# Graph network on one core: the last chunk of messages finished in three steps, the last block's sums added in PSUM

## The chip, the core and the metric

The kernel runs on one core of a Trainium2 chip. Its time is the device time of one execution in microseconds; before the change it is 4211.55 us, the median of three runs (4207.63 to 4215.61).

## What is computed

Four layers of a graph network on 6250 nodes with 64 features and 206250 edges, which come sorted by destination. Each layer normalises the node rows (mean, variance, ReLU) and adds its result to the rows `x`. The first two layers were left as they are. The change is in the third and at the seam between the third and the fourth.

```python
# third: messages along edges, averaged (as a power mean) at their destination
scale = sigmoid(mlp(E) @ Bw + Bb);  shift = mlp(E) @ Cw + Cb
M     = clip(scale * Vp[src] + shift, EPS) ** 2
x     = x + sqrt(segment_sum(M, dst) / max(count, 1))
# fourth: h = relu(layernorm(x)); three propagations with the same graph
embs = acc = h
for _ in range(3):
    embs = segment_sum(norm[:, None] * embs[row], col)
    acc  = acc + embs
x = x + acc / 4
```

## The kernel before

**Nodes and counts.** Nodes are padded to 49 blocks of 128, in seven chunks of seven blocks (`NB`, `CB`, `NC`). The graph stands in DRAM as a matrix of edge counts in fp8, one tensor `A[c]` for each chunk c of destination nodes: 128 partitions by 49 blocks of source nodes by 896 columns. A piece is 7 blocks of it, 784 KB. Node values go to TensorE as three bf16 parts each (`U3`: 128 x 49 x 3 x 64), so that their sum has nearly f32 precision; `split` makes the parts.

**The message stage** (lines 1383 to 1666). Edges are worked in 202 groups of 1024 (`G`), in a software pipeline of 208 slots: `slot(i)` starts group i (POOL gathers its source values by eight indirect DMAs, `fetched`), passes earlier groups through two small layers, gates, clips and squares group i-4, sums group i-5 by destination on TensorE, and adds group i-6 to the node sums `H` (`added_to_nodes`). Gathered values have four buffers; line 1559 of group i-4 frees the one that group i's gather fills. The order of PE, ScalarE and VectorE in this stage is the order of the program text; SP and POOL are ordered by the scheduler.

Beside this, each slot does some items of a list, `todo`, which `some_of` works off: (1) `crossed`, a comparison. It shows that the count matrix is symmetric: three or four 128 x 128 products turn blocks of a piece, and VectorE compares them with the mirrored piece (`there`) in line 1435. There are 392, 14 for each pair of chunks. (2) `partial`, a sum. It is a part of the first propagation of the fourth layer, done early: seven blocks of source nodes, already finished, are multiplied by 448 destination columns (`spread`, 21 products) and added to `Y` in line 1454. (3) `here`, the load of a piece one item ahead. Comparisons, sums and the squared messages (`p_m`, lines 1566 to 1638) share the two PSUM buffers `p_sum`. In slot i, n = ceil(items left / slots to the next end) items are done, n - n//2 ahead of `squared` and n//2 near the slot's end (lines 1620, 1621 and 1640). The ends are the slots in which chunks of nodes are complete: 35, 64, 93, 122, 151, 180 and 207.

Up to slot 35 the list holds four pairs of chunks (`FIRST`): 56 comparisons and 4 loads. When chunk c is complete, `finished(c)` averages, takes the root, adds to `X`, normalises, splits into `U3`, and then plans the next period (`CROSS[c]`): four pairs with 56 comparisons, and 14 sums over seven loads, 77 items. Chunk 5's period is slots 181 to 207. Chunk 6 plans nothing; it is finished in slot 207.

**The first propagation** (lines 1703 to 1715). Chunk 6's own part of the sums is done after the messages: for each of seven destination chunks, two sums of 21 products, two adds to `Y`, then seven f32 products (`to_nodes`, line 741) that turn `Y` into node rows, and `propagated`, five VectorE and two ScalarE instructions that scale the rows, add them to `H` and split them for the next pass.

**The second and third propagation** are `gather`: for each destination chunk 7 pieces, 343 products with 192 columns each (line 1195), four reductions and `propagated`. Six pieces are buffered. The product on piece k needs chunk k of the values split before.

Of the kernel before, what the change touches and what calls it, by code (L numbers as in the profile page):

```python
# [8 lines left out]
F32 = mybir.dt.float32  # L9
# [4 lines left out]
OP = mybir.AluOpType  # L14
AX = mybir.AxisListType

P = 128
N = 6250
D = 64
# [598 lines left out]
def fast(ctx, tc, bad, x, src, dst, edge_attr, W3, b3, W4, b4, w1, b1, w2, b2, Bw, Bb, Cw, Cb,  # L618
# [52 lines left out]
    missed = const.tile([P, 3], F32, name="missed")  # L671

    def blocks(c):
        return slice(c * CB, (c + 1) * CB)

    def over_features(v, n=CB):
        return v.unsqueeze(2).to_broadcast([P, n, D])
# [14 lines left out]

    def normed(h, X_c):

        m = stat.tile([P, CB], F32, name="m")
        nc.vector.tensor_reduce(m, X_c, axis=AX.X, op=OP.add)
        nc.vector.tensor_scalar_mul(m, m, 1.0 / D)
        nc.vector.tensor_sub(h, X_c, over_features(m))
        q = stat.tile([P, CB, D], F32, name="q")
        nc.vector.tensor_mul(q, h, h)  # L700
        v = stat.tile([P, CB], F32, name="v")
        nc.vector.tensor_reduce(v, q, axis=AX.X, op=OP.add)
        nc.scalar.activation(v, v, AF.Sqrt, bias=eps, scale=1.0 / D)
        nc.vector.reciprocal(v, v)
        nc.vector.scalar_tensor_tensor(h, h, 0.0, over_features(v), op0=OP.max, op1=OP.mult)

    def of_nodes(pool):

# [1 line left out]

    def split(u, U3, c):
        u3 = U3[:, blocks(c), :, :]
        nc.scalar.activation(u3[:, :, 0, :], u, AF.Copy)
        r = stat.tile([P, CB, D], F32, name="r")
        nc.vector.tensor_sub(r, u, u3[:, :, 0, :])
        nc.scalar.activation(u3[:, :, 1, :], r, AF.Copy)
        nc.vector.tensor_sub(u3[:, :, 2, :], r, u3[:, :, 1, :])
# [455 lines left out]

    def normed_and_split(h, U3, c, scale):
        normed(h, X[:, blocks(c), :])
        u = stat.tile([P, CB, D], F32, name="u")
        nc.vector.tensor_mul(u, h, over_features(scale[:, blocks(c)]))
        split(u, U3, c)

    def gather(apool, wpool, psum, U3, then, beside=iter(())):  # L1180


        zeros = wpool.tile([P, 6 * D], BF16, name="zeros", bufs=1)
# [1 line left out]
        for c in range(NC):  # L1185
            p = [psum.tile([P, 512], F32, name=f"p_acc{q}") for q in range(4)]
            for k in range(NC):
                t = apool.tile([P, CB, W], COUNT, name="piece")
                nc.sync.dma_start(t, A[c][:, blocks(k), :])
                for d in range(CB):  # L1190
                    if k == 0 and d % 2 == 0:
                        nc.tensor.matmul(p[d // 2][:, :6 * D], ident_b, zeros,
                                         start=True, stop=False)
                    for b in range(CB):
                        nc.tensor.matmul(  # L1195
                            p[d // 2][:, d % 2 * 3 * D:(d % 2 + 1) * 3 * D],
                            t[:, b, d * P:(d + 1) * P],
                            U3[:, k * CB + b, :, :].rearrange("p t f -> p (t f)"),
                            start=False, stop=(k == NC - 1 and b == CB - 1 and d in (1, 3, 5, 6)))
                for _ in range(2 - (c > 0 or k > 4)):  # L1200
                    next(beside, None)
# [181 lines left out]
    with ExitStack() as ph:  # L1383
# [10 lines left out]

        CROSS = (((0, 6), (0, 1), (0, 2), (0, 0)), ((1, 6), (1, 2), (1, 3), (1, 1)),
                 ((2, 6), (2, 3), (2, 4), (2, 2)), ((3, 6), (3, 4), (3, 5), (3, 0)),
                 ((4, 6), (4, 5), (4, 0), (4, 1)), ((5, 6), (5, 0), (5, 1), (5, 2)))
        FIRST = ((3, 3), (4, 4), (5, 5), (6, 6))
        unlike = cpool.tile([P, 28 * 2 * CB], F32, name="unlike")

        def order(pairs):
            ks = [k for _, k in pairs]
            return [(pairs[0][0], k)
                    for k in ks + [k for k in range(NC) if (pairs[-1][0], k) not in pairs]]

        here_of = list(FIRST) + [at for pairs in CROSS for at in order(pairs)]
        there_of = list(FIRST) + [at for pairs in CROSS for at in pairs]
        held = {}

        def here(n):  # L1410

            if n < len(here_of):
                i, k = here_of[n]
                t = held["here", i, k] = piece_pool.tile([P, CB, W], COUNT, name="piece")
                nc.sync.dma_start(t, A[k][:, blocks(i), :])

        def there(n):

# [23 lines left out]
        def partial(i, s):  # L1442

            t = held["here", i, s // 2]
            p = ps_a.tile([P, 512], F32, name="p_sum", bufs=2)
            for b in range(CB):
                spread(p, U3, i * CB + b, t[:, b, s % 2 * CW:(s % 2 + 1) * CW], CW,
                       i * CB, CB)

            def added():  # L1450
                if i == 0:
                    nc.vector.tensor_copy(Y[:, s, :], p[:, :CW])
                else:
                    nc.vector.tensor_add(Y[:, s, :], Y[:, s, :], p[:, :CW])

            return added

        todo, crossings, asked = [], [], []

        def plan(pairs, sums):  # L1460
            for at, (i, k) in enumerate(order(pairs) if sums else pairs):
                asked.append((i, k))
                todo.append((here, len(asked)))
                if at < len(pairs):
# [21 lines left out]
                if then:  # L1486
                    read.append(then)

        def finished(c):

            t = H[:, blocks(c), :]
            nc.vector.tensor_mul(t, t, over_features(n1[:, blocks(c)]))

            nc.vector.tensor_scalar_max(t, t, 1e-30)
            nc.scalar.activation(t, t, AF.Sqrt)
            nc.vector.tensor_mul(t, t, over_features(some[:, blocks(c)]))
            nc.vector.tensor_add(X[:, blocks(c), :], X[:, blocks(c), :], t)
            normed_and_split(H[:, blocks(c), :], U3, c, norm3)
            if c < NC - 1:
                plan(CROSS[c], True)  # L1500

        here(0)
        there(0)
        plan(FIRST, False)
        last = {b: g for g in range(G) for b, _, _ in halves(g)}
        ends = [last[c * CB + CB - 1] for c in range(NC)]

        BC_AT, M_AT, SUM_AT, ADD_AT = 3, 4, 5, 6
        of = [{} for _ in range(G)]
        ends = [e + ADD_AT for e in ends]

        def loaded(g):
            of[g]["e"] = mpool.tile([P, J * D], F32, name="e", bufs=6)
# [70 lines left out]
        def added_to_nodes(g):  # L1587
# [5 lines left out]
            for k, (b, q0, q1) in enumerate(halves(g)):  # L1593
# [4 lines left out]
                else:  # L1598
                    nc.vector.tensor_scalar(H[:, b, :], r, part, None, op0=OP.mult)
                    begun.add(b)  # L1600
            return [b // CB for b, _, _ in halves(g) if last[b] == g and b % CB == CB - 1]

        def slot(i):
            def at(later):
# [12 lines left out]
            read_them()  # L1617
            if at(1):
                layer(i - 1, w1_d, "eT", "p_1")
            n = -(-len(todo) // max(min(k for k in ends if k >= i) + 1 - i, 1))  # L1620
            some_of(n - n // 2)
            if at(M_AT):
                squared(i - M_AT)
# [16 lines left out]
            some_of(n // 2)  # L1640
            if at(SUM_AT):
                summed(i - SUM_AT)
            for c in done:
                finished(c)

        for g in range(4):
            loaded(g)
# [2 lines left out]
                slot(i)  # L1650
            read_them()

        assert not todo and len(crossings) == 28 * 2 * CB


        nc.vector.tensor_reduce(missed[:, 2:3], unlike, axis=AX.X, op=OP.add)
# [14 lines left out]
    with ExitStack() as ph:  # L1671
# [2 lines left out]
        psum = ph.enter_context(tc.tile_pool(name="ps4", bufs=1, space=PSUM, reuse_waits="tile"))  # L1674
        upool = ph.enter_context(tc.tile_pool(name="upool", bufs=1, reuse_waits="tile"))

        for layer in range(3):
            V3 = of_nodes((upool, node)[layer]) if layer < 2 else None

            def propagated(c, y):  # L1680
                z = wpool.tile([P, CB, D], F32, name="z")
                s3 = over_features(norm3[:, blocks(c)])
                nc.vector.tensor_mul(z, y, s3)
                if V3 is not None:
                    u = wpool.tile([P, CB, D], F32, name="u")
                    nc.vector.tensor_mul(u, z, s3)
                    split(u, V3, c)
                h = H[:, blocks(c), :]
                nc.vector.tensor_add(h, h, z)
                if V3 is None:  # L1690
                    o = X[:, blocks(c), :]
                    nc.vector.scalar_tensor_tensor(o, h, 0.25, o, op0=OP.mult, op1=OP.add)
                    lo, hi = c * W, min((c + 1) * W, N)
                    full = (hi - lo) // P
                    nc.sync.dma_start(
                        out[lo:lo + full * P, :].rearrange("(b p) f -> p b f", p=P),
                        o[:, :full, :])
                    if lo + full * P < hi:
                        nc.sync.dma_start(out[lo + full * P:hi, :], o[:hi - lo - full * P, full, :])

            if layer:
                gather(apool, wpool, psum, U3, propagated)
            else:
                for s in range(CS):
                    if s % 2 == 0:
                        whole = apool.tile([P, CB, W], COUNT, name="piece")
                        nc.sync.dma_start(whole, A[s // 2][:, blocks(NC - 1), :])
                    t = whole[:, :, s % 2 * CW:(s % 2 + 1) * CW]
                    p = psum.tile([P, 512], F32, name="p_sum", bufs=2)
                    for b in range(CB):  # L1710
                        spread(p, U3, NB - CB + b, t[:, b, :], CW, NB - CB, CB)
                    nc.vector.tensor_add(Y[:, s, :], Y[:, s, :], p[:, :CW])
                    if s % 2:
                        propagated(s // 2, to_nodes(
                            psum, Y[:, s - 1:s + 1, :].rearrange("p s w -> p (s w)"), CB))
            U3 = V3


def gnn_kernel(tc, *args):
# [38 lines left out]
```

## Time and profile before

| | us |
|---|---|
| median of three runs | 4211.55 |
| the profiled execution: time, span | 4226.45, 4224.1 |
| graph, degrees, first two layers: to the first gated group | 1054.6 |
| message stage, first gated group to the end of chunk 6's finish | 1054.6 to 3764.9 |
| first propagation's last part | 3764.3 to 3809.6 |
| second and third propagation | 3809.6 to the end |
| busy: PE, VectorE, ScalarE, POOL | 3145.3, 2075.1, 1238.6, 1611.6 |

Times of stages are counted from the span's start. The engines are named as the profile has them: PE and PEld are TensorE's products and weight loads, DVE is VectorE, ACT is ScalarE, POOL is GpSimd, SP issues most DMAs. In the page's groups a row gives line, engine, operation, output and inputs, how many; then busy time and the mean ns of one; then the idle time of the engine just ahead of them and what ended it.

### The profile page before, as it was taken

The page shows a single profiled execution, that of the slowest core. Times are in us where ns is not written, and L with a number is a line of the kernel's source. Part 1 is how long each engine was busy: PE and PEld are TensorE (multiplying, and loading weights), DVE is VectorE, ACT ScalarE, POOL GpSimd, SP SyncE. Part 2 cuts the span into 40 slices and gives each one's busy share as a digit, 9 for nine tenths or more (in the row PEclk, how much of TensorE's full clock was granted, in tenths as well). Part 3 has the DMA queues.
Part 4 walks back from the last instruction along what each step waited for, and adds up shares of the span by engine and source line. Part 5 has one row for each costly group of instructions (what it writes and reads, how often), then busy time and mean ns, then how long its engine had stood idle before and what let it go on. Part 6 is the DMA issues. An engine that isn't in the chain of part 4 may idle for free.

```text
span 4224.1 us, 60998 instructions
## 1 busy us (share of the span) xinstructions
PE 3145.3 (74%) x24478; PEld 2248.4 (53%) x24478; DVE 2075.1 (49%) x5101; ACT 1238.6 (29%) x2061; POOL 1611.6 (38%) x1894
## 2 busy tenths in 40 slices
PE   2899989996665666766676676766766766689999
PEld 1788889994333333333333343433333333359999
DVE  6999935322544554454545454545444444562111
ACT  3677700001333322332323232323332332320000
POOL 5000010003666655655555554555555655510000
PEclk9999999997777778777777777778778777889999
DMA  3244376552222222222222222212222222125664
GB/s 114 58 105 105 89 224 192 195 178 94 60 58 59 57 60 64 54 61 66 55 71 59 55 56 76 56 50 63 70 54 69 57 59 61 44 97 185 199 199 154
DMA packets 229380, 388.83 MB, mean 92 GB/s; under 512 B 93801, under 2 KB 139801, under 8 KB 228830
## 3 DMA queue, kind: packets, MB, share of 16 engines
q1 hardware_dynamic: 170478, 322.28, 24.6%
q0 software_dynamic: 55104, 60.65, 7.1%
q8 instruction: 194, 3.18, 0.3%
q10 hardware_dynamic: 3504, 1.90, 0.2%
q14 instruction: 100, 0.82, 0.1%
HBM read 340.48 MB, written 44.21 MB: 91 GB/s over the span
## 4 chain that ended last, share of the span: by engine, by line
PE 45%; DVE 22%; another core or an unknown queue 13%; issue 10%; ACT 7%; DMA 1%; POOL 1%; DVEq 0%; ACTq 0%; POOLq 0%
PE p_acc L1195 18%; PE p_bc L1549 6%; PE p_sum L750 5%; PE p L1535 4%; DVE to L1574 3%; ACT h L1539 2%; DVE hd L888 2%; DVE m L1559 2%; DVE lo L888 2%; DVE m L1560 2%; DVE junk L1435 2%; PE p_s L1582 2%; PE p_sum L1429 2%; PE p_bc L1545 2%
## 5 line engine op out<-in xcount | busy, mean ns | idle before, releaser
L1523 POOL DMA_INDIRECT v<-Vp_dram,src_g x1616 | 1539.4, 953 | 1511.1 <-DVE m L1559 700.3
L1195 PE MATMUL p_acc<-U,piece 128*128 128x192 bf16 x9604 | 816.1, 246 | 8.9 <-DMA piece<-A 8.9
L1195 PEld LDWEIGHTS <-piece 128*128 128x128 fp8e4 x9604 | 797.5, 98 | 21.0 <-DMA piece<-A 9.2
L1549 PE MATMUL p_bc<-BC,h 128*128 128x256 f32 x1616 | 580.5, 488 | 41.7 <-issue 40.7
L1429 PE MATMUL p_sum<-ident_b,piece 128*128 128x128 bf16 x1372 | 165.5, 246 | 511.4 <-DVE m L1638 233.0
L1429 PEld LDWEIGHTS <-piece 128*128 128x128 fp8e4 x1372 | 115.9, 110 | 679.3 <-issue 412.4
L1435 DVE SCALAR_TENSOR_TENSOR junk<-p_sum,there 128x512 bf16<-128x512 f32 (+1 forms) x392 | 242.4, 618 | 473.8 <-remote 324.8
L1549 PEld LDWEIGHTS p_bc<-BC,h 128*128 128x128 f32 x1616 | 338.2, 231 | 208.7 <-issue 173.0
L1559 DVE TENSOR_TENSOR m<-p_bc,v 128x512 f32<-128x512 f32 x202 | 139.7, 692 | 588.0 <-ACT p_bc L1554 479.0
L750 PE MATMUL p_sum<-piece,U 128*64 128x448 fp8e4 x2058 | 286.3, 391 | 122.6 <-issue 99.4
L1539 ACT ACTIVATE h<-p,b_c 128x512 f32<-128x512 f32 x404 | 263.9, 693 | 265.4 <-PE p_sum L1429 112.8
L1535 PE MATMUL p<-h,w_d 128*128 128x512 f32 x404 | 271.2, 751 | 91.4 <-ACT h L1539 67.9
L907 ACT ACTIVATE strip<-p_a 128x784 fp8e4<-128x784 f32 x392 | 301.3, 821 | 102.2 <-PE p_a L903 86.7
L1205 DVE TENSOR_REDUCE zg<-p_acc 128x128 f32<-128x384 f32 x112 | 56.3, 507 | 527.5 <-PE p_acc L1195 526.9
L1574 DVE TENSOR_SCALAR to<-count,lane 128x128 bf16<-128x128 bf16 x1616 | 288.1, 271 | 0.0
L1545 PE MATMUL p_bc<-BC_b,ones 3*128 3x512 bf16 x404 | 181.9, 450 | 134.8 <-DVE m L1560 122.0
L750 PEld LDWEIGHTS <-U 128*64 128x64 bf16 x2058 | 130.1, 118 | 278.5 <-issue 209.0
L1569 ACT ACTIVATE p_sum<-m 128x512 f32<-128x512 f32 x202 | 120.5, 597 | 537.9 <-DVE junk L1435 271.4
L1545 PEld LDWEIGHTS <-ones 3*128 3x128 bf16 x404 | 37.5, 93 | 411.5 <-issue 211.4
L1535 PE MATMUL p<-eT,w_d 128*128 128x512 f32 x404 | 243.4, 685 | 10.9 <-issue 6.5
L1568 ACT ACTIVATE m<-m 128x512 bf16<-128x512 f32 x202 | 127.2, 629 | 404.9 <-DVE m L1561 312.9
L1042 PE MATMUL p_sum<-U,strip 128*128 128x192 bf16 x2401 | 229.9, 247 | 0.0
(215 smaller groups left out, 3637.2 us busy)
## 6 DMA issues: line engine op xcount, KB each, us to landing
piece<-A SPq DMA_DIRECT2D x249, 784.0 KB
e<-in_edge_attr SPq DMA_DIRECT2D x202, 256.0 KB
v<-Vp_dram,src_g POOLq DMA_INDIRECT x1616
A<-strip SPq DMA_DIRECT2D x7, 3136.0 KB
there<-A SPq DMA_DIRECT2D x28, 784.0 KB
A<-strip SPq DMA_DIRECT2D x7, 2352.0 KB
pairs<-pair SPq DMA_DIRECT2D x1, 1616.0 KB
Vp_dram<-v SPq DMA_DIRECT2D x7, 224.0 KB
```

Of the source, the lines that this page charges most:

```text
L750: nc.tensor.matmul(p[half * D:(half + 1) * D, :w], U3[:, b, k, :], at_block, start=(i < 2), stop=(i >= 3 * n - 2))
L907: nc.scalar.activation(strips[s][:, :, col:col + 2 * SG].rearrange("p b (j l) -> p b j l", l=2), p[:, :, :2 * NB].rearrange("p j (b l) -> ...
L1042: nc.tensor.matmul(p[:, d * 3 * D:(d + 1) * 3 * D], strips[s][:, b, (d0 - lo + d) * P:(d0 - lo + d + 1) * P], U3[:, b, :, :].rearrange("p ...
L1195: nc.tensor.matmul(p[d // 2][:, d % 2 * 3 * D:(d % 2 + 1) * 3 * D], t[:, b, d * P:(d + 1) * P], U3[:, k * CB + b, :, :].rearrange("p t f - ...
L1429: nc.tensor.matmul(p[:, a - a0, :], held["here", i, k][:, a, b * P:(b + 1) * P], ident_b, start=True, stop=True)
L1435: nc.vector.scalar_tensor_tensor(junk[:, :(a1 - a0) * P], p[:, :a1 - a0, :].rearrange("p a q -> p (a q)"), 15.5, of_there, op0=OP.min, op1 ...
L1523: nc.gpsimd.indirect_dma_start(out=v[:, j, :], out_offset=None, in_=Vp_dram[:, :], in_offset=bass.IndirectOffsetOnAxis(ap=src_g[:, g, j:j ...
L1535: nc.tensor.matmul(of[g][p], w, of[g].pop(x), start=True, stop=True)
L1539: nc.scalar.activation(of[g][t], of[g].pop(p), **how)
L1545: nc.tensor.matmul(p_bc[:, 4 * b:4 * b + 4].rearrange("p j o f -> p (j o f)"), ones, BC_b, start=True, stop=False)
L1549: nc.tensor.matmul(p_bc[:, 2 * q:2 * q + 2].rearrange("p j o f -> p (j o f)"), h2[:, q * P:(q + 1) * P], BC, start=False, stop=(k == 1))
L1574: nc.vector.tensor_scalar(to[:, j, :], count, lane[:, g, j:j + 1], None, op0=OP.is_equal)
```

## The change

1. **Comparisons.** The four pairs of chunk 5 leave its period and join `FIRST`: there, 112 comparisons and 8 loads are planned for slots 0 to 35, and chunk 5's period has 14 sums and 7 loads.
2. **Three steps.** Chunk 6 is finished as 4, 2 and 1 blocks (`SPANS`), in slots 196, 205 and 207. `finished`, `normed` and `split` take a number of blocks. Two slots after the first of these, the sums of the four blocks are planned (14 sums of 12 products, 7 loads) up to slot 205; those of the two blocks (14 sums of 6 products, 7 loads) fall into slot 207, all of them. A period is now planned at the start of the slot after the finish, before n is worked out, not at its end.
3. **The last block.** Its rows of all seven count tensors are loaded into one piece buffer by seven DMAs. `with_the_rest` makes node values of the first propagation: for each block one f32 product of `Y` and three products of counts with the last block's three parts, all added up in one PSUM bank; `propagated` follows.
4. **Interleaving.** These node values are a generator that the second pass's `gather` advances once a piece: chunks 0 and 1 ahead of piece 0, chunk k+2 ahead of piece k+1. The order of PE and VectorE in the second pass is now that of the text. In `propagated` the add to `H` stands before the split.

In the built program, the scheduler places three of the second pass's piece loads on SP between the loads of two-block pieces; the seven loads of the last block come after them.

```diff
     def normed(h, X_c):
-        m = stat.tile([P, CB], F32, name="m")
+        n = X_c.shape[1]
+        m = stat.tile([P, CB], F32, name="m")[:, :n]
...
-    def gather(apool, wpool, psum, U3, then, beside=iter(())):
+    def gather(apool, wpool, psum, U3, then, beside=iter(()), ahead=iter(())):
...
                 nc.sync.dma_start(t, A[c][:, blocks(k), :])
+                next(ahead, None)
...
-                 ((4, 6), (4, 5), (4, 0), (4, 1)), ((5, 6), (5, 0), (5, 1), (5, 2)))
-        FIRST = ((3, 3), (4, 4), (5, 5), (6, 6))
+                 ((4, 6), (4, 5), (4, 0), (4, 1)), ())
+        FIRST = ((3, 3), (4, 4), (5, 5), (6, 6), (5, 6), (5, 0), (5, 1), (5, 2))
+        SPANS = [(c * CB, CB) for c in range(NC - 1)] + [(NB - CB, 4), (NB - 3, 2), (NB - 1, 1)]
...
+        summed_of = [at for i, pairs in enumerate(CROSS) for at in order(i, pairs)]
+        here_of = [(i, k, CB) for i, k in list(FIRST) + summed_of]
+        here_of += [(b0, k, n) for b0, n in SPANS[NC - 1:-1] for k in range(NC)] + [None]
...
+                if here_of[n] is None:
+                    held["rest"] = t
+                    for k in range(NC):
+                        nc.sync.dma_start(t[:, k, :], A[k][:, NB - 1, :])
+                    return
...
-            for b in range(CB):
-                spread(p, U3, i * CB + b, t[:, b, s % 2 * CW:(s % 2 + 1) * CW], CW,
-                       i * CB, CB)
+            b0, rows = (i * CB, CB) if i < NC else (i, dict(SPANS)[i])
+            for b in range(rows):
+                spread(p, U3, b0 + b, t[:, b, s % 2 * CW:(s % 2 + 1) * CW], CW, b0, rows)
...
-        ends = [e + ADD_AT for e in ends]
+        ends = [e + ADD_AT for e in ends[:-1]] + [G + ADD_AT - 3]
+        planned = {}
...
-            n = -(-len(todo) // max(min(k for k in ends if k >= i) + 1 - i, 1))
+            for args in planned.pop(i, ()):
+                plan(*args)
+            n = -(-len(todo) // max(min([k for k in ends if k >= i] or [i]) + 1 - i, 1))
...
-            for c in done:
-                finished(c)
+            for b0, n in done:
+                finished(b0, n)
+                if n == CB:
+                    planned[i + 1] = [(b0 // CB, CROSS[b0 // CB], True)]
+                elif b0 < NB - 1:
+                    planned[i + 2] = [(b0, (), True)]
...
+        def with_the_rest(V3):
+            y = Y.rearrange("p s w -> p (s w)")
+            for c in range(NC):
+                p = psum.tile([P, 512], F32, name="p_node", bufs=2).rearrange("p (b f) -> p b f", f=D)
+                for k in range(CB):
+                    d = slice((c * CB + k) * P, (c * CB + k + 1) * P)
+                    nc.tensor.matmul(p[:, k, :], y[:, d], twice, start=True, stop=False)
+                    for t in range(3):
+                        nc.tensor.matmul(p[:, k, :], held["rest"][:, c, k * P:(k + 1) * P],
+                                         U3[:, NB - 1, t, :], start=False, stop=(t == 2))
+                propagated(V3, c, p[:, :CB, :])
+                if c:
+                    yield
...
+        with tc.manual_schedule(engines={ET.PE, ET.DVE}):
+            gather(apool, wpool, psum, U1, second, ahead=with_the_rest(U1))
+        gather(apool, wpool, psum, U2[0], lambda *args: propagated(None, *args))
```

## The prediction

> **What bounds the kernel now.** I read the page first. Its slices show that the change touches two places: the message stage (TensorE clock at 7 or 8 tenths, no engine above 7 tenths), and the place near the end where PE returns to 9. The row for line 1523 then says who waits for whom in the message stage: POOL, which issues 1616 gathers, stands idle about as long as it works, and 700 us of that end with VectorE's line 1559, which frees a gather buffer.
>
> ```profile
> L1523 POOL DMA_INDIRECT v<-Vp_dram,src_g x1616 | 1539.4, 953 | 1511.1 <-DVE m L1559 700.3
> L1435 DVE SCALAR_TENSOR_TENSOR junk<-p_sum,there 128x512 bf16<-128x512 f32 (+1 forms) x392 | 242.4, 618 | 473.8 <-remote 324.8
> ```
>
> So nothing is full, and busy time does not tell what a comparison or a partial sum costs there. I therefore counted slots. Line 1569 runs once a slot on ScalarE; a table by windows, restricted to that line, gives elapsed time, its busy time and, in brackets, the slots.
>
> ```profile
> 1054.50:1297.50 243.00, 11.86 (x20) 0.75 0.24 64
> 1297.50:1443.80 146.30, 7.00 (x12) 0.76 0.21 55
> 1443.80:1701.70 257.90, 11.39 (x19) 0.79 0.22 58
> 1701.70:1750.20 48.50, 2.41 (x4) 0.71 0.19 44
> 1750.20:1816.40 66.20, 2.95 (x5) 0.80 0.30 84
> 3437.40:3490.00 52.60, 2.39 (x4) 0.73 0.18 41
> 3490.00:3658.60 168.60, 7.22 (x12) 0.79 0.20 54
> ```
>
> Set the division of the work list that stands in the code (items left over slots left) beside it. Slots 4 to 23 have two items each: 12.15 us a slot. Slots 24 to 35 have one: 12.19, although one of them ends chunk 0. Slots 36 to 54 have three, nearly all comparisons: 13.57; the same stretch of the five full periods is 1285.1 us for 95 slots, 13.53. Slots 55 to 58, two comparisons again: 12.13. Slots 59 to 63, two items, mostly sums of seven blocks: 13.24. So up to two comparisons a slot are free, under a floor set by POOL (fetches start 1.25 us apart, so 16 of them are 20.0 of the 24.3 us of two slots, and the rest is its wait for line 1559), and a third costs 1.4 us.
>
> Last, the chain of waits around 3750 us shows the seam.
>
> ```profile
> 3751.90 2.21 PE p_sum L750 x21
> 3754.14 0.62 DVE Y L1454
> 3754.76 0.54 DVE H L1492
> ...
> 3764.27 0.64 DVE U L717
> 3764.95 6.49 PE p_sum L750 x40
> 3771.44 0.81 PE p_node L741 x6
> ...
> 3773.79 3.90 PE p_sum L750 x38
> 3777.69 0.81 PE p_node L741 x6
> ```
>
> Chunk 6's finish takes 10.2 us on VectorE and ScalarE; then PE is the bound through seven rounds of 6.24 us, until the second pass starts at 3809.6. From there PE is never idle.
>
> **Part 1: comparisons moved forward (the loss).** Four tile pairs, 56 comparisons and their loads, move from slots 181 to 205 to the list worked off in slots 0 to 35. It goes from 60 items to 120: four a slot in slots 0 to 11, three in slots 12 to 35.
> - Slots 12 to 35: 24 x (13.53 - 12.15) = **+33 us**.
> - Slots 4 to 11, four items, of which no slot of the trace has any. Lower end: no more than the third, 8 x 1.4 = 11. Upper: each further comparison costs twice its VectorE time of 0.7 us and a turn of the two p_sum buffers, some 2.8 in place of 1.1, 8 x 4.2 = 33. I take 13.53 + 1.1, since the fourth falls into the slot's second half, where nothing of the gate chain waits for the buffer: 8 x 2.5 = +20.
> - Slots 0 to 3 fill the pipeline and POOL paces them: 0 to 4, taken 2.
> - Chunk 0's finish is hidden in slot 35 now (12.19 above); chunk 1's slot, in a full period, takes 27.9 us, and its neighbours return half of that, so a finish shows some 8. With cover gone, +5 (0 to 8).
>
> Sum **+60** (25 to 85). Added loads on SP's queue, a piece and a "there" per 14 comparisons, come at the rate of the later periods, so the 13.53 contains them.
>
> **Part 2: slots 181 to 197 (a gain).** Chunk 5 is left with its 14 sums and 7 loads, 21 items. Before, these 16 slots take 52.6 + 168.6 = 221.2 us, 13.83 each. After, five slots of two items at 13.24 and eleven of one item at the floor, 12.15: 5 x 0.59 + 11 x 1.68 = 21.4. Less 2 for finishing four blocks in such thin slots (0 to 8): **-19**.
>
> **Part 3: slots 198 to 206.** Fourteen four-block sums (12 matmuls of 0.105 us, 1.26) take the place of comparisons and of six seven-block sums (2.2 us each) in the draining slots 203 to 206, where PE works 14.4 of 15.1 us. Two of the 2.2 + 2.2 pairs become single 1.26 ones: 6.3, taken -6. In slots 198 to 202 two such sums stand for three comparisons, more PE, less VectorE: +2 (-3 to +6).
>
> **Part 4: the seam.** Measured from the end of line 1638 of the last message (3748.57): before, 61.0 us to the second pass. After, one after the other:
> - a Y add 0.6, then blocks 46 and 47 are finished: the same fourteen VectorE and four ScalarE instructions on 128 columns. The row of L1591 (192 columns, 0.353) and of L1596 (64 columns, 0.278) put one near 0.3: 5.5 us. PE waits for this; behind it in VectorE's order stands the last message's reduce.
> - slot 207: all fourteen two-block sums. PE needs 0.63, VectorE's add 0.62, with two buffers and handoffs 0.75 each: 10.5, and 0.6 for the last message.
> - block 48: eighteen narrow instructions, 4.8 us, with PE idle: the first node value's products wait for it, and in PE's order the whole second pass stands behind them.
> - chunks 0 and 1 of node values: per block one f32 product (two halves of 0.137, the rounds above) and three 64-column products, 14 x (0.274 + 3 x 0.056) = 6.2; then 0.8 until chunk 0 is split (3.9 us of chain less the 3.1 of chunk 1).
> - the other five chunks, between the second pass's products: 35 x 0.442 = 15.5. Their VectorE work (five instructions of 0.62 a chunk) hides under 4.1 + 3.1 us of PE.
>
> That is 44.5 us. Where the three products are priced matters: the Trainium skill ("TensorE: Matmul & The Clock Gate", section "LDWEIGHTS (loading the stationary operand)") gives columns / 1.2, 107 ns for each 128-column weight load, 147 x 0.107 = 15.7 us. Here line 1429, with fp8 weights of that size, starts three products within 0.17 us (3 in 0.33 us, the last of which is 0.22), 56 ns each: 8.2 us. I take the row.
>
> The same page (section "HAM oscillation — how this bites in real kernels") warns against PE gaps above 3.4 us. That speaks against this change: it has two (5.5 and 4.8 us) for today's one. Today's 7 us gap did cost:
>
> ```profile
> 3759.50:3769.70 10.20, 5.91 (x28) 0.50 0.21 86
> 3769.70:3809.60 39.90, 39.90 (x359) 1.00 0.38 122
> ```
>
> (PE's windows: length, busy, granted clock, DMA.) The 41 matmuls behind it took 7.15 us in place of 4.3. By the rule both gaps bring the half clock, +2.5 and +4; by the row only gaps of 7 us, +0. I take the rule: 51 us, **-10**. The ends are +2 and -20.
>
> On SP fourteen more issues come (0.33 us each); the first gather pieces stand among the two-block loads and wait for freed buffers, but DMA moved 420 GB/s here, a piece in 1.9 us, and seven loads of the last block have some 8 us. POOL's queue is not passed.
>
> **Sum.** +60 - 19 - 6 + 2 - 10 = **+27 us**. The profiled run took 4226.45 (span 4224.1), 15 above the median; there it is 4253. On the median, 4211.55 + 27 = **4238.5**.
>
> **Rivals.**
> 1. The comparisons are absorbed: from one item to two cost nothing, and if the floor of 12.15 also covers three and four, part 1 is +5 and the time 4211.5 + 5 - 33 = **4184**. For it: equal 12.15 and 12.19. Against it: five periods at 13.53 with the same instructions. It decides where slots 0 to 35 lose less than the 33 us that the rest returns. Chance 0.15.
> 2. Loss and gains nearly balance: the fourth item costs no more than the third (33 + 11), pipeline fill and chunk 0's finish stay hidden, and gaps of 5 us do not halve the clock (seam -16.5): 44 - 19 - 6 + 2 - 16.5 = +4.5, **4216**. For it: slot 207's PE work keeps the gaps apart. Against it: 27.9 us for a slot with a finish. Chance 0.12.
> 3. The change doesn't do what it says: finishes with their gaps only replace the old rounds and the seam gains nothing, and a fourth comparison costs 4.2 (+13 in part 1): 73 - 19 - 6 + 2 = +50, **4262**. For it: two long chains in VectorE's one order. Against it: rounds of 6.24 us that shrink to 3.1. Chance 0.20.
>
> My forecast has the remaining 0.53. The range is 4198 to 4276; the likeliest case alone spans 4220 to 4256. A measurement tells about 0.2% (8.4 us) from no change: slower 0.73, same 0.11, faster 0.16.
>
> **What would show it.** Right: slots 4 to 35 at 13.5 us or more, that is some 440 us in place of 389; slots 186 to 196 near 12.15; two PE gaps of about 5 us ahead of the node values; rounds of 3.1 us; the second pass unbroken. Wrong: a first stretch at 12.15 (rival 1), or slot 207 far longer than 11 us because a two-block load lands late.

## The result, and the profile after

The changed kernel takes **4252.07 us** (median of four runs, 4243.88 to 4257.4), the kernel before, run beside it, 4211.61. The ratio is 1.0081, with a 95% interval of 1.0056 to 1.0106: the change costs 40 us, between 24 and 45. The forecast was +27 us and slower. The profiled run of the changed kernel took 4249.28 us, its span 4247.4.

The rows that answer to those shown before, from the page's groups. The message stage's lines stand twelve further down (1523 is now 1535, 1435 is 1447, 1559 is 1571, 1569 is 1581):

```profile
L1535 POOL DMA_INDIRECT v<-Vp_dram,src_g x1616 | 1538.0, 952 | 1556.1 <-DVE m L1571 744.7 <-issue 439.8 <-DMA e<-in_edge_attr 343.9
L1447 DVE SCALAR_TENSOR_TENSOR junk<-p_sum,there 128x512 bf16<-128x512 f32 (+1 forms) x392 | 242.6, 619 | 533.3 <-remote 397.0 <-PE p_bc L1561 41.8 <-PE p_sum L1441 35.1
```

The work is the same (1616 fetches, 392 comparisons, the same mean times). Only the idle time has grown: POOL waits 44 us longer for the line that frees its buffers (744.7 in place of 700.3).

The slots again: windows restricted to the line that runs once a slot, with elapsed time, ScalarE's time in that line, and in brackets the slots. The windows are slots 4 to 11, 12 to 23, 24 to 35, 36 to 54, 59 to 64, 65 to 180, 181 to 185 and 186 to 196.

```profile
1066.70:1172.90 106.20, 4.81 (x8) 0.76 0.28 80
1172.90:1336.50 163.60, 7.19 (x12) 0.77 0.22 60
1336.50:1503.50 167.00, 7.18 (x12) 0.77 0.23 62
1503.50:1756.30 252.80, 11.39 (x19) 0.76 0.24 62
...
1804.70:1892.20 87.50, 3.53 (x6) 0.79 0.30 82
1892.20:3484.10 1591.90, 69.35 (x116) 0.77 0.23 60
3484.10:3549.60 65.50, 2.93 (x5) 0.80 0.26 73
3549.60:3702.80 153.20, 6.41 (x11) 0.76 0.21 51
```

Where the time went, each stretch beside the same stretch of the kernel before, in us:

| stretch | before | after | difference | forecast |
|---|---|---|---|---|
| start to the first gated group | 1054.6 | 1066.8 | +12.2 (5 of it ahead of the stage) | +2 |
| slots 4 to 11 | 97.0 | 106.2 | +9.2 | +20 |
| slots 12 to 35 | 292.3 | 330.6 | +38.3 | +38 |
| slots 36 to 180 | 1993.5 | 1980.6 | -12.9 | 0 |
| slots 181 to 197 | 232.8 | 226.0 | -6.8 | -19 |
| slots 198 to 204 | 75.0 | 73.5 | -1.5 | -4 |
| seam: end of the last message's line 1638 (now 1653) to the end of the third pass's products | 467.3 | 452.8 | -14.5 | -10 |

The column of differences adds up to 24, and the two spans are 23.3 apart; the medians are 40 apart. The fourth row is what wanders between executions of one kernel, as the first experiment shows. The seam's row holds: in five other profiles of kernels with the three steps, from the runs below, it takes 452.7 to 455.4, in two with the old seam 463.7 and 464.0.

The seam, in the changed kernel's timeline of PE (start, length, line, tile, how many; in brackets the idle time before it and what ended it):

```profile
3786.30 2.45 PE L751 MATMUL p_sum<-piece,U 128*64 128x448 fp8e4 x12 [4.15 <-DVE m L1653]
...
3793.52 1.44 PE L1594 MATMUL p_s<-m,to 128*128 128x192 bf16 x8 [3.55 <-DVE H L1608]
3794.89 6.51 PE L751 MATMUL p_sum<-piece,U 128*64 128x448 fp8e4 x48
3802.66 1.33 PE L751 MATMUL p_sum<-piece,U 128*64 128x448 fp8e4 x12 [1.26 <-DMA piece<-A]
3804.59 1.33 PE L751 MATMUL p_sum<-piece,U 128*64 128x448 fp8e4 x12 [0.60 <-DMA piece<-A]
...
3811.25 0.21 PE L1727 MATMUL p_node<-U,piece 128*128 128x64 bf16 x1 [3.49 <-ACT U L714]
...
3812.72 0.67 PE L1725 MATMUL p_node<-twice,Y 128*128 128x64 f32 x2
...
3813.36 0.67 PE L1725 MATMUL p_node<-twice,Y 128*128 128x64 f32 x2
...
3826.93 0.25 PE L1727 MATMUL p_node<-U,piece 128*128 128x64 bf16 x3
3827.02 0.41 PE L1725 MATMUL p_node<-twice,Y 128*128 128x64 f32 x2
...
3827.36 0.41 PE L1725 MATMUL p_node<-twice,Y 128*128 128x64 f32 x2
```

It shows a gap of 4.15 us ahead of the last four-block sum, where the forecast had none, the two finishes with PE idle (3.55 us for blocks 46 and 47 ahead of the last group's sum, 3.49 for block 48), slot 207's sums, two of which wait for their counts from DRAM (1.9 us together), and the node values twice: from one block's f32 product to the next it takes 0.64 us in chunk 0 (3812.72 to 3813.36), 0.34 us in a later chunk (3827.02 to 3827.36). The windows of PE's busy time (length, busy time and count, granted clock, DMA share and rate) say why:

```profile
3786.20:3789.60 3.40, 3.29 (x18) 0.51 0.01 2
...
3793.10:3796.50 3.40, 2.98 (x18) 0.50 0.00 0
3796.50:3810.10 13.60, 9.24 (x80) 1.00 0.83 274
3810.10:3823.80 13.70, 12.17 (x88) 0.50 0.37 149
3823.80:3850.00 26.20, 26.20 (x346) 1.00 0.39 124
```

The rows of 0.5 follow the gaps of 4.15 and 3.55 us and begin within that of 3.49: PE runs at half the clock for 3.4 us twice and for 13.7 us the third time.

### The profile page after: what moved, and what is told of

The parts are those of the page before. It is cut to its first block, busy times and chain, and to the rows that moved or that the text cites. A ratio compares the mean times of both kernels' runs of the same rounds, so it can differ in the third digit from the quotient of the medians.

```text
span 4247.4 us, 61300 instructions
## 1 busy us (share of the span) xinstructions
PE 3154.9 (74%) x24583; PEld 2257.2 (53%) x24583; DVE 2089.7 (49%) x5143; ACT 1241.8 (29%) x2071; POOL 1609.9 (38%) x1894
## 3 DMA queue, kind: packets, MB, share of 16 engines
q1 hardware_dynamic: 173070, 325.49, 24.7%
## 4 chain that ended last, share of the span: by engine, by line
PE 34%; DVE 14%; another core or an unknown queue 12%; issue 9%; ACT 6%; POOL 0%; DMA 0%; DVEq 0%; ACTq 0%; POOLq 0%
PE p_acc L1198 9%; PE p_bc L1561 6%; PE p_sum L751 5%; PE p L1547 5%; DVE to L1586 3%; PE p_s L1594 3%; DVE junk L1447 2%; ACT h L1551 2%; DVE m L1571 2%; DVE m L1572 2%; PE p_bc L1557 2%; PE p_e L1543 2%; PE p_sum L1441 2%; DVE p_sum L1641 1%
## 5 line engine op out<-in xcount | busy, mean ns | idle before, releaser
L1535 POOL DMA_INDIRECT v<-Vp_dram,src_g x1616 | 1538.0, 952 | 1556.1 <-DVE m L1571 744.7
L1561 PE MATMUL p_bc<-BC,h 128*128 128x256 f32 x1616 | 569.6, 479 | 46.1 <-issue 44.0
L1594 PE MATMUL p_s<-m,to 128*128 128x192 bf16 x1616 | 225.6, 297 | 24.3 <-issue 15.1
L889 DVE TENSOR_TENSOR lo<-count,key 128x4096 bf16<-128x4096 bf16 (+1 forms) x103 | 224.5, 2179 | 0.0
```

Of the source, the lines that this page charges most:

```text
L1535: nc.gpsimd.indirect_dma_start(out=v[:, j, :], out_offset=None, in_=Vp_dram[:, :], in_offset=bass.IndirectOffsetOnAxis(ap=src_g[:, g, j:j ...
L1561: nc.tensor.matmul(p_bc[:, 2 * q:2 * q + 2].rearrange("p j o f -> p (j o f)"), h2[:, q * P:(q + 1) * P], BC, start=False, stop=(k == 1))
L1594: nc.tensor.matmul(p, to[:, j, :], m3[:, j].rearrange("p t f -> p (t f)"), start=(j == 0), stop=(j == J - 1))
```

## The experiments

### The kernel before once more

No edit. 

> The kernel before, profiled a second time, to see how far two profiles of one kernel differ by stage. Slots 4 to 35 near 389 us, slots 36 to 180 within 15 us of 1993.5 us, slots 181 to 197 near 233 us. If slots 36 to 180, which the change does not touch, differ by more than 10 us between the two profiles, then the -13 us seen there between before and after is no effect of the change.

4204.76 us. The windows of slots 4 to 11, 12 to 23, 24 to 35 and 65 to 180 in this execution:

```profile
1058.60:1155.30 96.70, 4.74 (x8) 0.71 0.23 61
1155.30:1300.80 145.50, 7.13 (x12) 0.75 0.25 66
1300.80:1447.00 146.20, 6.99 (x12) 0.72 0.22 55
...
1846.00:3419.30 1573.30, 69.34 (x116) 0.78 0.23 62
```

Slots 4 to 35 repeat within 1 us; slots 65 to 180 took 1573.3 us here and 1593.0 in the profile of the prediction. So a difference in the first stretch can be read from two profiles, one in the long middle only if it is well over 20 us.

### The comparisons moved, nothing else

In the kernel before:

```diff
-        FIRST = ((3, 3), (4, 4), (5, 5), (6, 6))
+        FIRST = ((3, 3), (4, 4), (5, 5), (6, 6), (5, 6), (5, 0), (5, 1), (5, 2))
...
-                 ..., ((5, 6), (5, 0), (5, 1), (5, 2)))
+                 ..., ())
```

> The kernel before with one part of the change: chunk 5's 56 comparisons move to slots 0 to 35; chunk 6 is finished at once as before. My theory (a comparison above two in a slot costs): slots 0 to 35 lose 50 to 60 us, as in the changed kernel, and chunk 5's period, with 21 items over 27 slots, falls from 13.8 to the floor of 12.15 and returns 20 to 30; total +25 to +35 us. Rival (the loss in slots 0 to 35 comes from elsewhere in the change, for instance from narrower tiles): total below 0, about -25. Second rival, from the trace of the changed kernel, where slots 186 to 196 stay at 13.9 with one item each (sums are what costs there, not the number of items): the period returns nothing, total +45 to +55.

4248.45 us against 4214.34, ratio 1.0085 (1.0052 to 1.0118): +34. Slots 4 to 11, 12 to 23, 24 to 35, 181 to 185 and 186 to 196:

```profile
1065.10:1176.30 111.20, 4.81 (x8) 0.75 0.27 77
1176.30:1341.40 165.10, 7.18 (x12) 0.77 0.22 58
1341.40:1512.90 171.50, 7.18 (x12) 0.76 0.23 61
3493.50:3553.00 59.50, 2.91 (x5) 0.83 0.21 53
3553.00:3693.50 140.50, 6.41 (x11) 0.79 0.22 57
```

447.8 us in place of 389.3 in slots 4 to 35 (+58.5), and 200.0 in place of 221.2 in slots 181 to 196 (-21.2). The list's move alone makes the kernel slower by nearly as much as the whole change does (40), as the first expectation had it; both rivals named there are out.

### The three steps, the comparisons left where they were

In the changed kernel, the same two lines put back. 

> The changed kernel with the comparisons left in chunk 5's period, which now ends at slot 196 with 77 items in 16 slots, five a slot. Slots 0 to 35 return to 389 us. If each further comparison costs 1.1 us or more, slots 181 to 196 take 16 us each, 35 us more than before, and with the seam's 15 us gained the total is +15 to +25 us. If only the step from two items to more costs and their number doesn't (in the changed kernel slots of four took 13.3 us and slots of three 13.7), slots 181 to 196 stay near 13.8 to 14.3 and the total is -15 to -5 us, faster than both kernels.

4227.34 us, ratio 1.0024 (0.9999 to 1.0049): +13, hardly told from no change. Slots 4 to 35 are back at 388 us. Slots 181 to 185 and 186 to 196 now hold chunk 5's 56 comparisons and 14 sums in fewer slots, since the period ends at 196:

```profile
3444.70:3531.90 87.20, 3.01 (x5) 0.72 0.20 52
3531.90:3700.00 168.10, 6.60 (x11) 0.81 0.22 58
```

255.3 us in place of 221.2, 16.0 a slot, as the first of the two expectations had it. The seam takes 452.7 us here, so its gain is there, and the crowded period eats it: without room made for it, finishing earlier crowds the last period. Making the room in slots 0 to 35 costs no less. The move of the comparisons alone costs 34 us, the three steps alone 13 (0 to 21), both together 40.

### Six comparisons in a slot instead of four or three

In the changed kernel:

```diff
             n = -(-len(todo) // max(min([k for k in ends if k >= i] or [i]) + 1 - i, 1))
+            n = 6 if i < 20 else n
```

> The changed kernel with the 120 items of the first list worked off six to a slot in slots 0 to 19, and none in slots 20 to 35. If the cost lies in each comparison above two (1.1 us or more), slots 4 to 19 take 13.5 + 3 x 1.1 = 16.8 us or more, and the loss in slots 4 to 35 is 75 us or more in place of 47. If it lies in the slot that has more than two, whatever their number, slots 4 to 19 take 13.5 to 14.5 and slots 20 to 35 12.15, and the loss falls to 20 to 38 us.

4219.13 us, ratio 1.0017 (0.9993 to 1.0041). Slots 4 to 11, 12 to 23 and 24 to 35:

```profile
1068.50:1180.80 112.30, 4.81 (x8) 0.79 0.28 81
1180.80:1343.20 162.40, 7.14 (x12) 0.77 0.28 79
1343.20:1490.00 146.80, 7.00 (x12) 0.74 0.19 43
```

The same 120 items cost 32 us in place of 47.5. A slot of six comparisons takes about 14 us, hardly more than one of three (13.6 to 13.9), and the slots left empty return to 12.2. So between three and six comparisons the price is one of the slot, not of each comparison: the +1.1 us that the prediction put on the fourth is not there. For other items this doesn't hold: the slots of five in the run before, sums among them, took 15.5 us without the slot of the finish.

### One item ahead of the squares, the rest behind

If comparisons cost because they take the `p_sum` buffers ahead of the squares, moving them behind must help. In the changed kernel:

```diff
-            some_of(n - n // 2)
+            first = min(n, 1) if i < 36 else n - n // 2
+            some_of(first)
...
-            some_of(n // 2)
+            some_of(n - first)
```

> The changed kernel with, in slots 0 to 35, one item ahead of the squared messages and the rest at the slot's end, in place of two and one (or two and two). If what costs is that two comparisons ahead of the squares hold both p_sum buffers, so that ScalarE's squares wait for VectorE's compare, slots 12 to 35 fall from 13.8 to 12.2 and the loss in slots 4 to 35 from 47 us to 10 or less; the total is +0 to +10 against before. If what costs is the number of items in a slot, it stays at 40 us or more.

4250.33 us where the kernel before, on this chip, had a median of 4236.93: ratio 1.0027 (1.0008 to 1.0045). Slots 4 to 35 lose 37 us in place of 47.5, between the two expectations (10 or less, 40 or more). The buffers ahead of the squares are the smaller part of it, if the 10 us are not what two profiles differ by.

### At least six, or twelve, in every slot

In the changed kernel, the first line for six; the second for twelve; in the kernel before, the third:

```diff
+            n = max(n, 6) if i < 196 else n
...
+            n = max(n, 12) if i < 196 else n
...
+            n = max(n, 6)
```

> The changed kernel with at least six items a slot while the list holds any, in every period up to slot 195: 77 items in 13 slots, then 16 slots with none. If a slot with more than two items costs about 1.5 to 2 us whatever their number (six a slot in the first list: 13.7 us), a period of 29 slots takes 13 x 14.2 + 16 x 12.15 = 379 us in place of 400, and five periods and the first list return 100 + 15 us: about 4135 to 4160 us, faster than both kernels. If sums, which are longer on TensorE than comparisons, add up in a slot (six sums of seven blocks are 13 us of TensorE), the crowded slots take 17 us or more and the time is within 20 us of the kernel with six in the first list alone, 4200 to 4240.

> The same with at least twelve items a slot: 7 crowded slots a period, 22 with none. With a cost a slot, whatever the number, it is faster still, by 5 x 6 x 2 = 60 us against six. With a cost per item of 0.7 us of VectorE once the slot is full, a slot of twelve comparisons takes 12.15 + some 9 us and the period 7 x 21 + 22 x 12.15 = 414 us: 4250 us or more, slower than six a slot by 100.

> The kernel before, with its own lists and its finish of chunk 6 at once, and at least six items a slot in every period. Against the changed kernel with six a slot everywhere it shows what the three steps and the seam are worth when the comparisons no longer hide it: my reading of the traces says 15 us in favour of the three steps (seam 14.5, draining slots 2). Rival: the seam's gain is eaten when slots 186 to 196 hold sums only; then the two are within 5 us of each other.

Beside 4236.93 for the kernel before on this chip: with six **4124.23** us, ratio 0.9732 (0.9691 to 0.9774); with twelve 4262.36, ratio 1.0058 (1.0036 to 1.0080); the kernel before with six 4134.92, ratio 0.9727 (0.9695 to 0.9758). Six in a slot is worth 102 us to the kernel before and leaves the changed one 113 below it, more than twice what the change lost. A price per slot had given 4135 to 4160 for the first of the three. With six the change is no longer behind: the two versions with six, 10.7 us apart, can't be told apart, so the 15 us expected for the three steps are neither shown nor excluded. The changed kernel with six, slots 59 to 64 and 65 to 180 (94.2 and 1593.0 before, 87.5 and 1591.9 after the change alone):

```profile
1780.50:1853.20 72.70, 3.50 (x6) 0.73 0.20 44
1853.20:3365.20 1512.00, 68.58 (x116) 0.79 0.25 63
```

With twelve, slots 65 to 180 take 1607.4 us and slots 36 to 54 go from 252.8 to 276.5: a slot can also be too full. That is the second expectation, of a cost per item once the slot is full.

### What goes with a crowded slot: POOL's fetches broken up

The average of 12.15 us in thin slots hides an alternation. Line 1559 is the first VectorE instruction of a slot; its rows in the timeline of the kernel before:

```profile
1059.39 0.69 DVE L1559 TENSOR_TENSOR m<-p_bc,v 128x512 f32<-128x512 f32 x1 [1.05 <-ACT h L1539]
1076.27 0.69 DVE L1559 TENSOR_TENSOR m<-p_bc,v 128x512 f32<-128x512 f32 x1 [10.66 <-ACT p_bc L1554]
1083.54 0.69 DVE L1559 TENSOR_TENSOR m<-p_bc,v 128x512 f32<-128x512 f32 x1 [1.05 <-ACT p_bc L1554]
1100.61 0.69 DVE L1559 TENSOR_TENSOR m<-p_bc,v 128x512 f32<-128x512 f32 x1 [6.52 <-ACT p_bc L1554]
1107.88 0.69 DVE L1559 TENSOR_TENSOR m<-p_bc,v 128x512 f32<-128x512 f32 x1 [1.46 <-issue]
```

Slots of 7.3 and 17 us take turns, and the long one has about 10 us in which VectorE does nothing. POOL's rows in the same stretch show sixteen fetches without a break, from 1053.1, 1077.2 and 1101.6 us on: two groups. VectorE stands still in the second eight and takes up line 1559 again some 3.5 us after the last of them has ended:

```profile
1096.09 0.95 POOL L1523 DMA_INDIRECT v<-Vp_dram,src_g  x1 [0.30 <-issue]
1101.57 1.03 POOL L1523 DMA_INDIRECT v<-Vp_dram,src_g  x1 [4.54 <-DVE m L1559]
```

Counted from the traces between 1054 and 3700 us (a run of fetches ends where none starts for 2 us; the last three columns say where the time of the gaps lies):

| kernel | runs of 8 | runs of 16 | VectorE gaps over 5 us: number, sum | in the first eight of sixteen | in the second eight | in the break behind sixteen |
|---|---|---|---|---|---|---|
| before | 10 | 92 | 96, 837 us | 29 | 558 | 197 |
| after | 17 | 88 | 97, 828 us | 28 | 535 | 193 |
| after, six in a slot | 71 | 62 | 64, 695 us | 1 | 450 | 179 |
| before, six in a slot | 72 | 60 | 69, 748 us | 1 | 461 | 178 |
| after, twelve in a slot | 47 | 70 | 87, 884 us | 0 | 532 | 209 |

(A few runs of other lengths are left out.) In the kernel before, first and second eights fill about the same time, 934 and 894 us; the gaps take 3% of the one and 62% of the other. The number of runs alone doesn't tell the loss, though: with twelve in a slot there are fewer runs of sixteen than before, and more idle time.

In a slot of 7.3 us the next line 1559 has freed a buffer before POOL's eight fetches, 10 us, are over, so POOL goes on to sixteen. In most slots of six comparisons, 11 to 15 us, it hasn't; POOL pauses. That the runs come from two short-spaced lines 1559 is the reading of these rows; that they also cause the next long slot needs a test, since a stall with another cause would fall into the second eight as well.

For that, POOL was given something else to do after each group's eight fetches, in the kernel before, in the changed one, and in the changed one with six:

```diff
                     in_offset=bass.IndirectOffsetOnAxis(ap=src_g[:, g, j:j + 1], axis=0))
+            rest = mpool.tile([P, 256], BF16, name="rest", bufs=1)
+            for _ in range(4):
+                nc.gpsimd.iota(rest, pattern=[[1, 256]], base=0, channel_multiplier=0, ...)
```

and, as another way to it, the kernel before got three buffers for the fetched rows in place of four (`bufs=3`).

> The kernel before, with a pause on POOL after each group's eight fetches: four small iotas into a scratch tile, about 0.3 us each by the 238 ns of an iota of half the size in the profile, so 1.2 to 1.6 us with their gaps. Theory: the slots lose time because POOL fetches two groups without a break and the other engines stand still in the second eight; a break that is always there lets POOL fall behind by a little in each group, runs of sixteen fetches become few, and the stalls with them. Then the kernel before goes to 4120 to 4170, as it did with six comparisons in a slot. Rival: the length of the engines' own slot decides, POOL's break only adds to POOL's 10 us a group; then the stall in a pair of slots grows from 20 to about 23 us for POOL's two groups, and the time rises by up to 100 x 2.8 = 280 us (4300 to 4500).

> The changed kernel with the same pause. Theory: as above, and since slots 4 to 35 no longer have a stall that falls into their middle, the loss of the change there (47 us) goes too: 4120 to 4170, within 15 us of the kernel before with the pause. Rival: 4340 to 4540, and the two stay 40 us apart.

> The changed kernel with six comparisons in a slot at least, and the pause. Theory: nearly no run of sixteen is left in any slot (61 were, of 131 runs); each still cost some 10 us, so up to 300 us could go if nothing takes their place; POOL's own floor is then 11.3 to 11.6 us a slot, so slots 36 to 196 stay at or above 1870 in place of 1980: 4000 to 4100. Rival: 4124 or more.

> The kernel before, with three buffers for the fetched rows in place of four. If two buffers that come free close together are what lets POOL fetch sixteen in a row, one buffer less takes something from it: fewer runs of sixteen, 4130 to 4200. If only the spacing of line 1559 from one slot to the next decides, the count of buffers doesn't matter: 4200 to 4225, with the same runs of sixteen. If the fetched rows arrive too late with three, it is slower than 4230.

With the kernel before at 4238.01: the kernel before with the pause 4358.43 (1.0275, 1.0230 to 1.0320), the changed one with it 4356.93 (1.0272, 1.0223 to 1.0321), with six and the pause 4282.03 (1.0086, 1.0052 to 1.0120). None came near the 4120 to 4170 that the theory gave the first two, nor the 4000 to 4100 of the third; all three lie in the rival's range, and for its reason in part, since a break adds to POOL's own time (that the first two would stay 40 us apart, as the rival said, they did not). The pause was not the one I meant to give: POOL's order is the scheduler's, and it drew the iotas forward, so that groups up to about 2000 us got about ten of them, 4.1 to 4.5 us, and the later ones none. POOL itself, at 14 us a group, became the bound of that first part. The first slots, though, live on rows fetched ahead, and there the trace gives an answer. The same line of the kernel before with the pause:

```profile
1070.36 0.69 DVE L1563 TENSOR_TENSOR m<-p_bc,v 128x512 f32<-128x512 f32 x1 [0.97 <-ACT p_bc L1558]
1077.55 0.69 DVE L1563 TENSOR_TENSOR m<-p_bc,v 128x512 f32<-128x512 f32 x1 [0.97 <-issue]
1084.94 0.69 DVE L1563 TENSOR_TENSOR m<-p_bc,v 128x512 f32<-128x512 f32 x1 [0.97 <-ACT p_bc L1558]
1091.56 0.69 DVE L1563 TENSOR_TENSOR m<-p_bc,v 128x512 f32<-128x512 f32 x1 [0.83 <-issue]
1099.10 0.69 DVE L1563 TENSOR_TENSOR m<-p_bc,v 128x512 f32<-128x512 f32 x1 [0.82 <-ACT p_bc L1558]
1111.25 0.69 DVE L1563 TENSOR_TENSOR m<-p_bc,v 128x512 f32<-128x512 f32 x1 [5.87 <-DMA v<-Vp_dram,src_g]
```

and POOL beside it (the first rows that begin a run of iotas or of fetches):

```profile
1066.52 4.50 POOL L1528 IOTA rest<- 128x256 bf16 x11
1071.38 0.97 POOL L1523 DMA_INDIRECT v<-Vp_dram,src_g  x1 [0.36 <-DVE m L1563]
1081.10 4.08 POOL L1528 IOTA rest<- 128x256 bf16 x10
```

From 1058.3 to 1101.6 us six slots in a row take 6.7 to 7.5 us, with the same two items in each, while POOL fetches in eights. There is no 17. From 1111 us on VectorE waits openly for rows ("DMA v"), since POOL is late. So in this stretch the long slots of the kernel before are no work of the other engines: without the second eight of a run they are gone. The pause also thins the fetches out, 24 in these 44 us where the kernel before has 32 in 49; whether the break or the thinning does it, this run can't separate. How much of the time a pause of the right length would win was not shown, and POOL's own 10 us a group stay as a floor.

Three buffers: 4222.64, ratio 0.9966 (0.9944 to 0.9987), 90 runs of sixteen, and slots 4 to 35 at 392 us. The number of buffers doesn't decide the runs, as the second expectation had it.

**What stays open** is why the engines stand still then. The rows are not late: in all 202 groups of the kernel before, the last fetch had ended 30 to 55 us before line 1559 used them. ScalarE's rows in one of the long slots:

```profile
1088.93 0.69 ACT L1539 ACTIVATE h<-p,b_c 128x512 f32<-128x512 f32 x1
1098.50 0.69 ACT L1539 ACTIVATE h<-p,b_c 128x512 f32<-128x512 f32 x1 [8.88 <-remote]
```

The trace's semaphore records name this "remote": the wait ends at 1098.48 us with a raise of the semaphore that PE's instructions raise, and nobody else. So do all waits over 3 us that the profile puts down to "remote" between 1054 and 3700 us, 63 of VectorE (545 us) and 30 of ScalarE (205 us). But PE's last product before it has ended at 1091.59 by its record. Here the other engines wait for PE's word 7 us after its products seem done; in 30 of the 93 waits it comes over 3 us after PE's last product. The ends of products are modelled, so the trace doesn't tell whether PE itself was held or only its raise, nor what POOL's fetches have to do with it.

## Why the prediction was right, and where it was not

**The whole.** +27 us was forecast, 40 (24 to 45) measured, and the mechanism was the one named: the comparisons moved into slots 0 to 35 cost more than the rest returns. The run with that move alone has it without the rest. That the sum came so near is in part luck: the loss was 5 us smaller than forecast, the gain in slots 181 to 197 12 smaller, the gain at the seam 4 larger.

**What bounds the kernel.** "Up to two comparisons a slot are free, under a floor set by POOL" held as a count of slots and failed as an explanation. I read the 24.3 us of two slots as sixteen fetches and a wait. That is what POOL's rows show, but nothing in it makes 12.15 a floor for the other engines; broken into eights, six such slots take 7.3 while the rows fetched ahead last. Averages over 12 to 20 slots, the very view that I leaned on, covered the alternation of 7.3 and 17.

**Part 1**, +60 forecast. Slots 12 to 35, with chunk 0's finish: 38 forecast, 38.3 measured, by two errors that cancel. Slot 35, which has the finish, takes 18.1 us before and 18.8 after, so the 5 us put on lost cover are 0.7; the slots of three cost 37.6 together and not 33. Slots 4 to 11: 20 forecast, 9.2 measured; a slot of four takes 13.27 us, not 14.6. The term that was mis-sized is the fourth comparison, 1.1 us in the sum, nothing on the chip, and the run with six in a slot shows that further ones cost hardly more. The fill cost 7 us from the first fetch to the first gated group, not 2 (48.0 us in both profiles of the kernel before, 55.2 after). Together 54.7.

**Part 2**, -19 forecast, -6.8 measured. Slots 181 to 185 took 65.5 us, as forecast (5 x 13.24 = 66.2). Slots 186 to 195, each with one item, a load or mostly a seven-block sum, took 12.85 each and not 12.15, and 12.6 in the run with the comparisons moved, so a single sum is not quite as free as a single comparison. The larger miss is slot 196, which has the finish of four blocks: 24.7 us, where 12.15 + 2 was forecast. That one wanders: it is 15.6 in the runs with six in a slot up to 19 and with one item ahead of the squares, whose slots 181 to 197 are the same, so there this stretch came out 17.8 and 14.2 us shorter than in the kernel before. The slots of the full finishes show two lengths as well, 18 to 21 or 26 to 29 us. The -19 was thus near what these two executions show, and the size of the gain is known to some 10 us only.

**Part 3**, -4 forecast, -1.5 measured: too small to say more.

**Part 4**, -10 forecast, -14.5 measured. The finishes were right: blocks 46 and 47 took 5.5 us (forecast 5.5), block 48 4.6 (4.8). Slot 207's fourteen sums took 12.4 us in place of 10.5, because two of its loads came 1.9 us late, in SP's order between pieces of the second pass: the danger that the prediction named last, in a small size. The last message's reduce and products ahead of them took 2.7, at half the clock, in place of 0.6. The half clock came, as the Trainium skill's rule of gaps above about 3.4 us has it ("TensorE: Matmul & The Clock Gate", section "HAM oscillation — how this bites in real kernels") and against the row of 7 us gaps: gaps of 3.49, 3.55 and 4.15 us were enough here, three of them where the prediction had two. It made chunks 0 and 1 take 14 x (0.64 - 0.34) = 4.2 us more; forecast 4. The gain over the forecast is the later node values: three products of 64 columns follow each other within about 0.09 us, 29 ns apart at full clock. The row that I chose, 56 ns, was for products of 128 columns. The 107 ns of the same page (section "LDWEIGHTS (loading the stationary operand)") are the length of one weight load, and the 15.7 us estimated from it took that length for the spacing: line 1195's loads of 128 fp8 columns last 98 ns each in the profile, and those of line 1727 start 29 ns apart. 35 blocks at 0.34 in place of 0.442 us are the missing 4 us. The second and third pass ran unbroken: less the five chunks of node values (2.3 us each) they take 407.1 us, 406.3 before.

**The bookkeeping.** Measured by these parts, the change costs 54.7 - 6.8 - 1.5 - 14.5 = 32 us, within the interval (the 5 us ahead of the stage are left out). The spans are only 23 apart because slots 36 to 180, which the change leaves alone, were 12.9 us shorter in the second profile, as they were 21 us shorter in a second execution of the kernel before.

## What to carry to other kernels

A stage that repeats in slots should be looked at slot by slot before an average of it is called a floor: two alternating lengths can mean that something is released in pairs. The price of side work in such a pipeline can belong to the slot it falls in more than to the item; try it crowded into few slots and spread thin before moving it elsewhere (here at least six at a time won 102 us, twelve, in the changed kernel, lost 25, and moving such items lost 34). When a step is finished early to shorten a seam, count what its earlier end crowds in the period before it.

## What was not expected of the hardware

When POOL issues sixteen indirect fetches without a break, VectorE stands still in the second eight and just behind it: 755 of the 837 us of its gaps over 5 us in the kernel before lie there, some 8 us for each of 92 runs, and 29 us in the first eights. ScalarE and PE stand with it (8.88 and 7.65 us in the stretch shown above). A break of 4 us after every eight, filled with other POOL instructions, left six slots in a row free of it. The waits that the profile calls "remote" end with PE's semaphore, up to 8.7 us after PE's last product has ended by its record; the cause is not known.
